# The first image's start: the constants' arithmetic in pieces between x's statistics and transforms, early loads reordered, three Newton steps

## The chip, the cores and the metric

One core of one Trainium2 chip. The metric is the device time of one execution in microseconds; lower is better.

## The reference

The input x has 8 images of 8 channels of 256 x 256 float32 values; the channels form 4 groups of 2. Two layers follow one another:

```python
x = x + fno(group_norm(x))       # 4 Fourier layers between pointwise convolutions
x = x + dilate3x3(group_norm(x)) # maximum over a 3 x 3 window, border -2
```

The Fourier network lifts each group from 2 channels (and 2 coordinate planes) to 10 with a pointwise convolution fc0; runs four layers, each of which adds a spectral convolution (a real 2D FFT, of which only 24 x 12 modes are kept and mixed by complex weights, and the inverse) to a grouped 10 x 10 pointwise convolution; applies `h * sigmoid(h * softplus(beta)) / 1.1` after the first three; and ends with fc1 (128 hidden channels per group), the same swish, and fc2. The group norm divides by `sqrt(var + 1e-5)`, taken over each group of an image. All parameters are inputs of the kernel, so what depends on them alone (softplus of the betas, products of fc0 with the first layer's weights, weights scaled by softplus) is computed on the chip at the start of each execution. That part is called the constants here.

## The kernel before, in words

The Fourier transforms are matrix products with small tables of sines and cosines, so TensorE (PE) does nearly everything: per image, four layers of 11 chunks (`burst` and `transform`), then fc1 and fc2 in 128 steps (`first`, `second`). ScalarE (ACT) applies Silu and copies out of PSUM, VectorE (DVE) transposes, sums and mixes modes, GpSimd (POOL) and SyncE (SP) issue DMAs.

The order of the work on PE, DVE, ACT and SP is written out by hand: inside `tc.manual_schedule` (L931) each of these engines executes its instructions in program order. The pieces of work are Python generators; a `yield` is a place where work of another image can be put between. While an image is in its layers, the head (fc1, fc2) and the tail (`dilate`) of the image before are woven in. The first image has no predecessor, so nothing is woven into its start.

What comes before L931 (the loads L85 to L116, the memsets, the constants L139 to L205) is ordered by a scheduler, which also weaves it into the first instructions of the part written by hand.

The start of an image is `start` (L686): `spectrum_x`, then `mix` for layer 0. For the first image, in order:

- `load_x` (L76, L78): x in two halves of 1 MB, tile `turned`, issued by SP at L85 ahead of all else. L86 to L116 load parameters and tables, some on SP's queue, most on POOL's. The tables that matter below: `grp` (group sums for the statistics of y), `fw` and `er` (transforms of x), `unf`, `fw8` and `stack` (transforms in the layers), `xe`, `wext`. After them SP issues three loads of spectral weights, tile t, 400 KB each (L409), and 44 loads of x in another layout into h (L541, 48 KB each).
- The constants: `softplus` (L139) is called for `beta_p` (4 columns) and `beta_a` (16 columns): an exponential and a logarithm on ACT with small DVE operations around them; `sp` is the softplus, `rs` its reciprocal over 1.1. Then `io` (L160 to L162), fc1's and fc2's weights w1 and w2 scaled (L163, L165), 24 recorded matmuls into `p_wc` (L171, L174), and from these and the softplus `wc` (L176, L179), `wm` (a second use of the tile `wbd`, L182, L184), `cv` (L186) and `cz` (L193 to L198); `wt` (L199) and `wext` (L202) scaled. `wt` is read by the bursts from layer 1 on, w1 and w2 by the head, `wext` by L355, `wc`, `wm` and `cz` at the end of `mix`.
- `spectrum_x` (L275): `bn_stats` of x on DVE, four groups of each half (L281); aggregation (L285); two group means by PE (tiles p_st_x, p_sv_x) with four small DVE operations between and one, L302, behind; the reciprocal square root (`rsqrt`, L258), which is an integer estimate and four Newton steps of three dependent DVE operations each (L263 to L265); x normalized group by group (L306); then matmuls with `er` (L318), a copy (L319), transposes (L324), a copy (L325), matmuls with `fw` (L331), copies (L334), matmuls with `unf` (L343), copies (L347), and on DVE the product with `wext` (L355) and a sum (L358).
- `mix` (L412): twelve large DVE operations (L420, L423) on the modes, small ones, matmuls `p_f` (L464), copies into `fz` (L474 to L480).
- `rows_even` (L483): matmuls `p_g` (L496); their copies into `zt` are shared by DVE and ACT (`copy_banks`, L215 and L217). Then the bursts of layer 0: L600, L606, Silu at L611, transposes at L550, `transform` at L567.

`rsqrt` serves the statistics of x (once an image) and of y (`stats_end`, L229, once an image). For the last image y's statistics and the final dilation (`dilate_last`, L747) come after the last matmul.

Of the kernel before, what the change touches and what calls it, by code (L numbers as in the profile page):

```python
# [21 lines left out]
G = 4  # L22
WID = 10
# [13 lines left out]
NO = 3  # L37
# [9 lines left out]
def fno_dilate_kernel(ctx: ExitStack, tc: tile.TileContext, a: dict, out: bass.AP):  # L47
    nc = tc.nc
    mm = nc.tensor.matmul
# [3 lines left out]
    const = ctx.enter_context(tc.tile_pool(name="const", bufs=1))  # L53
# [8 lines left out]
    def ps_tri(name):  # L62
        return ps.tile([128, 3, 512], F32, tag="tri", bufs=2, name=name)
# [5 lines left out]
    def part(i):  # L69
        return slice(32 * i, 32 * i + 32)  # L70
# [9 lines left out]
    def load(name, shape, eng=nc.gpsimd):  # L80
        t = const.tile(list(shape), F32, tag=f"c_{name}", name=f"c_{name}")
        eng.dma_start(t, a[name])
# [22 lines left out]
    nc.sync.dma_start(wext.rearrange("p g o j -> p (g o j)"), a["wext"].partition_broadcast(128))  # L105
# [7 lines left out]
    w1 = load("w1", (128, NBLK, HID))  # L113
    w2 = load("w2", (128, G, 47))
# [21 lines left out]

    def softplus(t, n, name):  # L139
        e = const.tile([128, n], F32, tag=f"{name}_e", name=f"{name}_e")  # L140
        nc.vector.tensor_scalar(e, t, -1.0, None, ALU.mult)
        nc.vector.tensor_tensor(e, e, t, ALU.max)
        nc.scalar.activation(e, e, AF.Exp, scale=-1.0)
        nc.vector.tensor_scalar(e, e, 1.0, None, ALU.add)
        nc.scalar.activation(e, e, AF.Ln)
        sp = const.tile([128, n], F32, tag=f"{name}_sp", name=f"{name}_sp")
        nc.vector.tensor_scalar(sp, t, 0.0, None, ALU.max)
        nc.vector.tensor_tensor(sp, sp, e, ALU.add)
        nc.vector.tensor_scalar(sp, sp, 1e-20, None, ALU.max)
        rs = const.tile([128, n], F32, tag=f"{name}_rs", name=f"{name}_rs")  # L150
        nc.vector.tensor_scalar(rs, sp, 1.1, None, ALU.mult)
        nc.vector.reciprocal(rs, rs)
        return sp, rs

    sp_p, rs_p = softplus(beta_p, 4, "bp")
    sp_a, rs_a = softplus(beta_a, 4 * G, "ba")
    io = const.tile([128, 4 * G], F32, tag="io", name="io")
    nc.vector.tensor_copy(io[:, 0:4], sp_a[:, 0:4])  # L160
    nc.vector.tensor_tensor(io[:, 4:12], sp_a[:, 4:12], rs_a[:, 0:8], ALU.mult)
    nc.vector.tensor_copy(io[:, 12:16], rs_a[:, 8:12])  # L162
    nc.vector.tensor_scalar(w1, w1, sp_p[:, 3:4], None, ALU.mult)  # L163
    for g in range(G):
        nc.vector.tensor_scalar(w2[:, g, :], w2[:, g, :], rs_a[:, 12 + g : 13 + g], None, ALU.mult)  # L165


    wc = const.tile([128, 32], F32, tag="wc", name="wc")
    p = ps_tri("p_wc")
    for g in range(G):  # L170
        mm(p[32 * g : 32 * g + 6, 0, :32], fc0x[part(g), :], wt[part(g), 0, g, :], start=True, stop=True)  # L171
    for i in range(2):
        for r in range(4):
            mm(p[part(r), 1, NO * G * i : NO * G * (i + 1)], fc0c[:, i, :], wbd[:, NO * r : NO * (r + 1), :],  # L174
               start=True, stop=True)
    nc.vector.memset(wc, 0.0)  # L176
    for g in range(G):
        gs = slice(32 * g, 32 * g + 6)
        nc.vector.tensor_scalar(wc[gs, :], p[gs, 0, :32], sp_p[gs, 0:1], None, ALU.mult)  # L179

    wm = wbd
    nc.vector.memset(wm, 0.0)  # L182
    for g in range(G):
        nc.vector.tensor_scalar(wm[32 * g : 32 * g + 2, :WID, g], wc[32 * g : 32 * g + 2, :WID], -1.0, None, ALU.mult)  # L184
    cv = const.tile([128, 2, NO, G], F32, tag="cv", name="cv")
    nc.vector.tensor_tensor(  # L186
        cv.rearrange("p i o g -> p (i o) g"), p[:, 1, : 2 * NO * G].rearrange("p (i g) -> p i g", g=G),
        sp_a[:, 0:4].unsqueeze(1).to_broadcast([128, 2 * NO, G]), ALU.mult,
    )


    for i, l in enumerate((0, 2)):
        nc.vector.tensor_tensor(  # L193
            cz[:, i], cz[:, i], sp_a[:, 4 * l : 4 * l + 4].unsqueeze(1).to_broadcast([128, NO, G]), ALU.mult,
        )
    nc.vector.tensor_tensor(cz[:, 0], cz[:, 0], cv[:, 0], ALU.add)
    nc.vector.tensor_copy(cz[:, 2], cv[:, 1])
    nc.vector.tensor_scalar(cz1, cz1, sp_p[:, 1:2], None, ALU.mult)  # L198
    nc.vector.tensor_tensor(  # L199
        wt, wt, io.rearrange("p (l g) -> p l g", l=4).unsqueeze(3).to_broadcast([128, 4, G, 32]), ALU.mult,  # L200
    )
    nc.vector.tensor_tensor(  # L202
        wext.rearrange("p g o j -> p g (o j)"), wext.rearrange("p g o j -> p g (o j)"),
        io[:, 0:4].unsqueeze(2).to_broadcast([128, G, 5 * WID]), ALU.mult,
    )  # L205


    alone = [True]

# [48 lines left out]
    def rsqrt(v, r, d):  # L258

        nc.vector.tensor_scalar(r.bitcast(I32), v.bitcast(I32), -0.5, float(0x5F3759DF), ALU.mult, ALU.add)  # L260
        nc.vector.tensor_scalar(v, v, -0.5, None, ALU.mult)
        for _ in range(4):
            nc.vector.tensor_tensor(d, r, r, ALU.mult)  # L263
            nc.vector.tensor_tensor(d, d, v, ALU.mult)
            nc.vector.scalar_tensor_tensor(r, d, 1.5, r, ALU.add, ALU.mult)  # L265
# [663 lines left out]

    stats_of = {}  # L930
    with tc.manual_schedule(engines={PE, DVE, ACT, SP}):  # L931
        d = {}
        for _ in start(0, d):
            pass
        for b in range(n_img):
            stored = [dram.tile([128, NQ * PIX], F32, tag=f"hs{c}", name=f"stored_{b}_{c}") for c in range(NCH)]
            nxt, new, n_ready = {}, None, 0
# [19 lines left out]
            d = nxt  # L957
# [178 lines left out]
```

## Time and profile before

| | |
|---|---|
| median of three runs | 3673.78 us (3665.64, 3673.78, 3674.04) |
| profiled execution | 3669.94 us |
| span of the profile | 3668.1 us |
| mean granted PE clock | 0.979 of full |
| PE busy | 3478.0 us, 95% |
| ACT busy | 2865.8 us, 78% |
| DVE busy | 2388.5 us, 65% |
| x's statistics (L281) on DVE | 9.76 to 16.43 us |
| normalization of x (L306) starts | 26.08 us |
| first burst of layer 0 (L600) starts | 57.79 us |

The table gives times from the start of the span. In the profile a row of the timeline is: start, busy time, engine, line, operation, tiles written and read, their shapes, how often; in brackets the time for which the engine stood idle just before, and what ended that. A wait for several things is put down to the last of them. A row of stages gives from:to, length, then the busy time and count of PE, its weight loads, DVE, ACT and POOL, then the granted PE clock as a share of full speed, the share of the DMA engines and GB/s.

### The profile page before, as it was taken

Reading aid. Unit: us, or ns where it says so; the run is one execution under the profiler, and the core shown is the slowest. Engines: PE = TensorE matmul, PEld = TensorE weight load, DVE = VectorE, ACT = ScalarE, POOL = GpSimd, SP = SyncE. Lnnn points to the kernel's source line nnn. Section 1 sums busy time; section 2 is a strip of 40 time slices with the busy share of each in tenths; the row PEclk is TensorE's granted clock in tenths of the full one; section 3 lists DMA queues with packets and bytes.
Section 4 is the critical chain, followed back from the end, with each engine's and each line's share of the span. In section 5 each row is a group of like instructions: output and inputs, shape, how many; then the busy total and the mean of one; then the engine's idle time right before and its main releaser. Section 6 shows DMA issues by size and latency. Waiting matters only on the chain.

```text
span 3668.1 us, 112640 instructions
## 1 busy us (share of the span) xinstructions
PE 3478.0 (95%) x50872; PEld 1269.3 (35%) x50872; DVE 2388.5 (65%) x3711; ACT 2865.8 (78%) x3021; POOL 117.0 (3%) x202
## 2 busy tenths in 40 slices
PE   5768999999999999999999999999999999999997
PEld 2323333333333333333333333333333333333222
DVE  6776666557775677756776577766777567772443
ACT  2435888888788888787888888888878888879986
POOL 1000000000000000000000000000000000000000
PEclk7879999999999999999999999999999999999998
DMA  3006111442225312271214512253222531225221
GB/s 92 16 16 213 50 50 47 154 119 72 71 87 191 86 52 66 91 223 56 67 56 136 170 56 78 61 174 110 73 72 84 192 85 54 64 70 190 85 81 48
DMA packets 114081, 344.71 MB, mean 94 GB/s; under 512 B 15985, under 2 KB 18481, under 8 KB 98177
## 3 DMA queue, kind: packets, MB, share of 16 engines
q1 hardware_dynamic: 95392, 276.32, 24.8%
q0 software_dynamic: 18208, 61.18, 5.1%
q8 instruction: 400, 6.55, 0.7%
q14 instruction: 81, 0.66, 0.1%
HBM read 213.44 MB, written 123.74 MB: 92 GB/s over the span
## 4 chain that ended last, share of the span: by engine, by line
PE 74%; DVE 15%; issue 5%; ACT 4%; DMA 2%; POOL 0%; ACTq 0%; DVEq 0%; POOLq 0%
PE p_fc L842 20%; PE p_fc L825 20%; PE p_z L606 9%; PE p_d L567 7%; PE p_z L603 7%; PE p_z L600 3%; DVE turned L550 3%; PE p_u L585 3%; DVE y L851 3%; DVE S L423 2%; DVE turned L420 2%; DMA yin<-y_rows 2%; DVE turned L381 1%; PE p_g L518 1%; PE p_b L390 1%
## 5 line engine op out<-in xcount | busy, mean ns | idle before, releaser
L827 ACT ACTIVATE act<-p_fc 128x1536 f32<-128x1536 f32 x1024 | 1493.0, 1458 | 3.1 <-PE p_fc L825 3.1
L825 PE MATMUL p_fc<-hs,c_w 32*128 32x512 f32 x8192 | 1133.3, 626 | 29.8 <-DVE y L851 10.0
L842 PE MATMUL p_fc<-act,c_w 128*32 128x512 f32 x8192 | 1007.5, 599 | 0.2 <-ACT act L827 0.2
L826 ACT ACTIVATE act<-p_fc 128x512 f32<-128x512 f32 x1024 | 616.3, 602 | 214.1 <-PE p_fc L825 201.5
L550 DVE STREAM_TRANSPOSE turned<-h 128x1024 f32<-128x1024 f32 x528 | 632.4, 1225 | 179.0 <-ACT h L611 178.4
L611 ACT ACTIVATE h<-p_z 128x512 f32<-128x512 f32 (+1 forms) x528 | 511.9, 1021 | 205.0 <-PE p_z L606 204.9
L851 DVE TENSOR_TENSOR y<-p_fc,y 128x512 f32<-128x512 f32 x392 | 267.9, 683 | 524.9 <-PE p_fc L842 524.9
L825 PEld LDWEIGHTS p_fc<-hs,c_w 32*128 32x128 f32 x8192 | 356.6, 183 | 602.0 <-ACT act L826 259.2
L842 PEld LDWEIGHTS p_fc<-act,c_w 128*32 128x32 f32 x8192 | 222.5, 109 | 704.7 <-issue 330.7
L606 PE MATMUL p_z<-c_binv,zt 32*128 32x256 f32 x5632 | 410.4, 405 | 0.0
L606 PEld LDWEIGHTS p_z<-c_binv,zt 32*128 32x128 f32 x5632 | 259.3, 186 | 307.5 <-issue 294.4
L603 PE MATMUL p_z<-h,c_wt 32*32 32x512 f32 x8448 | 357.0, 602 | 7.9 <-ACT act L826 4.2
L567 PE MATMUL p_d<-turned,c_fw 32*32 32x480 f32 (+1 forms) x9216 | 308.9, 541 | 0.7 <-DVE turned L550 0.4
L575 ACT ACTIVATE turned<-p_d 128x1440 f32<-128x1440 f32 x144 | 182.9, 1270 | 90.9 <-PE p_d L567 87.6
L613 ACT ACTIVATE h<-p_z,c_bias 128x512 f32<-128x512 f32 (+1 forms) x176 | 186.5, 1110 | 71.7 <-PE p_z L606 71.5
L215 ACT ACTIVATE zt<-p_g 128x198 f32<-128x198 f32 (+2 forms) x118 | 53.6, 576 | 182.1 <-PE p_g L496 98.4
L423 DVE TENSOR_REDUCE S<-turned 128x80 f32<-128x800 f32 x192 | 189.0, 984 | 5.9
L420 DVE TENSOR_TENSOR turned<-t,B 128x800 f32<-128x800 f32 x192 | 188.7, 983 | 1.1
L567 PEld LDWEIGHTS p_d<-turned,c_fw 32*32 32x32 f32 x9216 | 127.3, 103 | 166.0 <-issue 65.0
L381 DVE STREAM_TRANSPOSE turned<-zt 128x960 f32<-128x960 f32 x96 | 177.2, 1873 | 2.5
L603 PEld LDWEIGHTS p_z<-h,c_wt 32*32 32x32 f32 x8448 | 93.2, 103 | 174.4 <-DVE y L851 48.8
L585 PE MATMUL p_u<-turned,c_stack 128*32 128x480 f32 (+1 forms) x1152 | 136.7, 543 | 11.5 <-DVE turned L574 6.2
(198 smaller groups left out, 1754.1 us busy)
## 6 DMA issues: line engine op xcount, KB each, us to landing
stored<-h SPq DMA_DIRECT2D x88, 1024.0 KB
hs<-stored SPq DMA_DIRECT2D x352, 256.0 KB
t<-in_spw SPq DMA_DIRECT2D x96, 400.0 KB
yin<-y_rows POOLq DMA_DIRECT2D x56, 512.0 KB, 5.1
h<-in_xp SPq DMA_DIRECT2D x352, 48.0 KB
turned<-in_xw SPq DMA_DIRECT2D x16, 1024.0 KB
y<-in_x SPq DMA_DIRECT2D x56, 256.0 KB
y_rows<-y POOLq DMA_DIRECT2D x56, 256.0 KB, 4.1
```

What stands on the lines that cost most here:

```text
L420: nc.vector.tensor_tensor(pr, sw[k], bt[:, k2, k].unsqueeze(2).to_broadcast([128, G, 2 * WID, WID]), ALU.mult)
L423: nc.vector.tensor_reduce(s[k2][:, k].rearrange("p s o g -> p (s o) g"), pr.rearrange("p g m i -> p m g i"), AX.X, ALU.add,)
L550: nc.vector.transpose(dst[:, 2 * i : 2 * i + 2], h[:, c, 2 * i : 2 * i + 2].rearrange("p f (s x) -> p f s x", s=2))
L567: mm(banks[q][part(v % 4), : 240 * n], fw8[part(q), v, :], t[part(q), :, :, v, : NBLK * WID], start=v < 4, stop=v >= 4)
L603: mm(o, wt[part(q), l, g, :], h[part(q), c, f, :], start=True, stop=False)
L606: mm(banks[q][:, HW * s : HW * (s + 1)], zt[part(q), 2 * c + s].rearrange("p f o -> p (f o)"), binv[part(q), :], start=False, stop=s == 1)
L611: nc.scalar.activation(dst, src, AF.Silu)
L825: mm(banks[g], w1[part(g), blk, :], hs[k][part(g), :], start=True, stop=True)
L826: nc.scalar.activation(act[:, 0, :], one, AF.Silu)
L827: nc.scalar.activation(act[:, 1:4, :], tri, AF.Silu)
L842: mm(acc[part(g), :], w2[:, g, 15 - rb - i : 47 - rb - i], act[:, g, :], start=i == 0, stop=i == 1)
L851: nc.vector.tensor_tensor(y, sums, y, ALU.add)
```

## The change

Three edits.

1. The loads of `grp`, `fw8` and `stack` on SP's queue move behind the load of `wext`; `fw` moves behind `er`. The other loads keep their order, and POOL's are untouched.
2. The constants become a generator `prepare` with eight pieces, executed inside the part written by hand. `start(0, d)` yields after each of its stages; after its yields 3, 6, 8, 10, 12, 14 and 16 one piece is issued, and the eighth after all of `start`. The arithmetic is the same; the two softplus run side by side, piece by piece.
3. `rsqrt` does three Newton steps in place of four, everywhere.

Where the yields lie: 3 after the aggregation L285; 6 after the operations behind p_st_x (L297); 8 after p_sv_x, the root, and the first group's normalization; 10 after the fourth group's; 12 after L319; 14 after L325; 16 after L334. The matmuls and small operations that follow each yield come behind the piece in the program.

The diff, its core:

```diff
-    grp = load("grp", (128, 128), nc.sync)
-    fw = load("fw", (128, 2, 32), nc.sync)
-    fw8 = load("fw8", (128, 8, 32), nc.sync)
-    stack = load("stack", (128, 32), nc.sync)
     fc0x = load("fc0x", (128, 6))
...
     er = load("er", (128, 2, 32), nc.sync)
+    fw = load("fw", (128, 2, 32), nc.sync)
     unf = load("unf", (128, 3, 32), nc.sync)
...
     nc.sync.dma_start(wext.rearrange("p g o j -> p (g o j)"), a["wext"].partition_broadcast(128))
+    fw8 = load("fw8", (128, 8, 32), nc.sync)
+    stack = load("stack", (128, 32), nc.sync)
+    grp = load("grp", (128, 128), nc.sync)
...
+    def prepare():
+
+        pair = ((beta_p, 4, "bp"), (beta_a, 4 * G, "ba"))
...
+        for i, (t, _, _) in enumerate(pair):
+            nc.vector.tensor_scalar(e[i], t, -1.0, None, ALU.mult)
+            nc.vector.tensor_tensor(e[i], e[i], t, ALU.max)
+        for i in range(2):
+            nc.scalar.activation(e[i], e[i], AF.Exp, scale=-1.0)
+        yield
+        for i, (t, _, _) in enumerate(pair):
+            nc.vector.tensor_scalar(e[i], e[i], 1.0, None, ALU.add)
+            nc.vector.tensor_scalar(sp[i], t, 0.0, None, ALU.max)
+        for i in range(2):
+            nc.scalar.activation(e[i], e[i], AF.Ln)
+        yield
+        p = ps_tri("p_wc")
...
+        yield
+        for i in range(2):
+            nc.vector.tensor_tensor(sp[i], sp[i], e[i], ALU.add)
+            nc.vector.tensor_scalar(sp[i], sp[i], 1e-20, None, ALU.max)
+            nc.vector.tensor_scalar(rs[i], sp[i], 1.1, None, ALU.mult)
+            nc.vector.reciprocal(rs[i], rs[i])
...
+        nc.vector.tensor_tensor(
+            wext.rearrange("p g o j -> p g (o j)"), wext.rearrange("p g o j -> p g (o j)"),
+            io[:, 0:4].unsqueeze(2).to_broadcast([128, G, 5 * WID]), ALU.mult,
+        )
+        yield
+        nc.vector.memset(wc, 0.0)
+        for g in range(G):
+            gs = slice(32 * g, 32 * g + 6)
+            nc.vector.tensor_scalar(wc[gs, :], p[gs, 0, :32], sp_p[gs, 0:1], None, ALU.mult)
+        yield
...
+        nc.vector.memset(wm, 0.0)
...
+        yield
...
+        nc.vector.tensor_scalar(cz1, cz1, sp_p[:, 1:2], None, ALU.mult)
+        yield
+        nc.vector.tensor_tensor(
+            wt, wt, io.rearrange("p (l g) -> p l g", l=4).unsqueeze(3).to_broadcast([128, 4, G, 32]), ALU.mult,
+        )
+        nc.vector.tensor_scalar(w1, w1, sp_p[:, 3:4], None, ALU.mult)
+        for g in range(G):
+            nc.vector.tensor_scalar(w2[:, g, :], w2[:, g, :], rs_a[:, 12 + g : 13 + g], None, ALU.mult)
+        yield
...
-        for _ in range(4):
+        for _ in range(3):
             nc.vector.tensor_tensor(d, r, r, ALU.mult)
...
-        d = {}
-        for _ in start(0, d):
-            pass
+        d, ready = {}, prepare()
+        for n, _ in enumerate(start(0, d), 1):
+            if n in (3, 6, 8, 10, 12, 14, 16):
+                next(ready)
+        next(ready)
```

More of the change, by code (lines that the diff above doesn't have):

```diff
@@ L135, in fno_dilate_kernel @@
     nc.vector.memset(dc, 0.0)
[L139 to L153, printed above, removed]
@@ L157, in fno_dilate_kernel @@
-    sp_p, rs_p = softplus(beta_p, 4, "bp")
-    sp_a, rs_a = softplus(beta_a, 4 * G, "ba")
-    io = const.tile([128, 4 * G], F32, tag="io", name="io")
[L160 to L165, printed above, removed]
@@ L168, in fno_dilate_kernel @@
-    wc = const.tile([128, 32], F32, tag="wc", name="wc")
[L169 to L179, printed above, removed]
+    io = const.tile([128, 4 * G], F32, tag="io", name="io")
@@ L181, in fno_dilate_kernel @@
+    wc = const.tile([128, 32], F32, tag="wc", name="wc")
     wm = wbd
-    nc.vector.memset(wm, 0.0)
-    for g in range(G):
-        nc.vector.tensor_scalar(wm[32 * g : 32 * g + 2, :WID, g], wc[32 * g : 32 * g + 2, :WID], -1.0, None, ALU.mult)
     cv = const.tile([128, 2, NO, G], F32, tag="cv", name="cv")
[L186 to L189, printed above, removed]
@@ L192, in fno_dilate_kernel @@
-    for i, l in enumerate((0, 2)):
+    def prepare():
+        pair = ((beta_p, 4, "bp"), (beta_a, 4 * G, "ba"))
+        e, sp, rs = [[const.tile([128, n], F32, tag=f"{name}_{k}", name=f"{name}_{k}") for _, n, name in pair]
+                     for k in ("e", "sp", "rs")]
+        for i, (t, _, _) in enumerate(pair):
[12 more added lines that the diff above has]
+        for g in range(G):
+            mm(p[32 * g : 32 * g + 6, 0, :32], fc0x[part(g), :], wt[part(g), 0, g, :], start=True, stop=True)
+        for i in range(2):
+            for r in range(4):
+                mm(p[part(r), 1, NO * G * i : NO * G * (i + 1)], fc0c[:, i, :], wbd[:, NO * r : NO * (r + 1), :],
+                   start=True, stop=True)
+        yield
+        for i in range(2):
+            nc.vector.tensor_tensor(sp[i], sp[i], e[i], ALU.add)
+            nc.vector.tensor_scalar(sp[i], sp[i], 1e-20, None, ALU.max)
+            nc.vector.tensor_scalar(rs[i], sp[i], 1.1, None, ALU.mult)
+            nc.vector.reciprocal(rs[i], rs[i])
+        (sp_p, sp_a), (_, rs_a) = sp, rs
+        nc.vector.tensor_copy(io[:, 0:4], sp_a[:, 0:4])
+        nc.vector.tensor_tensor(io[:, 4:12], sp_a[:, 4:12], rs_a[:, 0:8], ALU.mult)
+        nc.vector.tensor_copy(io[:, 12:16], rs_a[:, 8:12])
@@ L193, in fno_dilate_kernel @@
         nc.vector.tensor_tensor(
-            cz[:, i], cz[:, i], sp_a[:, 4 * l : 4 * l + 4].unsqueeze(1).to_broadcast([128, NO, G]), ALU.mult,
-        )
[L196 to L205, printed above, removed]
+            wext.rearrange("p g o j -> p g (o j)"), wext.rearrange("p g o j -> p g (o j)"),
@@ new lines, in prepare @@
+            io[:, 0:4].unsqueeze(2).to_broadcast([128, G, 5 * WID]), ALU.mult,
+        )
+        yield
[5 more added lines that the diff above has]
+        nc.vector.tensor_tensor(
+            cv.rearrange("p i o g -> p (i o) g"), p[:, 1, : 2 * NO * G].rearrange("p (i g) -> p i g", g=G),
+            sp_a[:, 0:4].unsqueeze(1).to_broadcast([128, 2 * NO, G]), ALU.mult,
+        )
@@ new lines, in prepare @@
+        nc.vector.memset(wm, 0.0)
+        for g in range(G):
+            gs = slice(32 * g, 32 * g + 2)
+            nc.vector.tensor_scalar(wm[gs, :WID, g], wc[gs, :WID], -1.0, None, ALU.mult)
+        yield
+        for i, l in enumerate((0, 2)):
+            nc.vector.tensor_tensor(
+                cz[:, i], cz[:, i], sp_a[:, 4 * l : 4 * l + 4].unsqueeze(1).to_broadcast([128, NO, G]), ALU.mult,
+            )
+        nc.vector.tensor_tensor(cz[:, 0], cz[:, 0], cv[:, 0], ALU.add)
+        nc.vector.tensor_copy(cz[:, 2], cv[:, 1])
@@ L208, in fno_dilate_kernel @@
+        nc.vector.tensor_scalar(cz1, cz1, sp_p[:, 1:2], None, ALU.mult)
+        yield
+        nc.vector.tensor_tensor(
+            wt, wt, io.rearrange("p (l g) -> p l g", l=4).unsqueeze(3).to_broadcast([128, 4, G, 32]), ALU.mult,
+        )
+        nc.vector.tensor_scalar(w1, w1, sp_p[:, 3:4], None, ALU.mult)
+        for g in range(G):
+            nc.vector.tensor_scalar(w2[:, g, :], w2[:, g, :], rs_a[:, 12 + g : 13 + g], None, ALU.mult)
+        yield
     alone = [True]
```

## The prediction

> **What bounds the kernel now.** I read the page first, to see how much of the span the change can reach, then the first 60 us in order of time on VectorE (DVE), then the waits of the SP queue, then the granted clock by stage. The page:
>
> ```profile
> span 3668.1 us, 112640 instructions
> PE 3478.0 (95%) x50872; PEld 1269.3 (35%) x50872; DVE 2388.5 (65%) x3711; ACT 2865.8 (78%) x3021; POOL 117.0 (3%) x202
> PE 74%; DVE 15%; issue 5%; ACT 4%; DMA 2%; POOL 0%; ACTq 0%; DVEq 0%; POOLq 0%
> ```
>
> TensorE bounds the whole. But at the front nothing else can run: image 0 has no earlier image to share engines with. PE's first large work, the bursts of layer 0, starts at 57.8 us, and until then the chain runs through DVE. The timeline of DVE, 9 to 27 us (start, busy us, line, tiles):
>
> ```profile
> 9.76 0.69 DVE L281 BATCH_NORM_STATS2 bn_x<-turned 128x6 f32<-128x512 f32 x1
> 11.19 0.16 DVE L148 TENSOR_TENSOR bp_sp<-bp_sp,bp_e 128x4 f32<-128x4 f32 x1 [0.75 <-ACT bp_e L145]
> 13.96 2.47 DVE L281 BATCH_NORM_STATS2 bn_x<-turned 128x6 f32<-128x512 f32 x4
> 16.34 0.41 DVE L285 BATCH_NORM_AGGREGATE mv_x<-bn_x 128x2 f32<-128x12 f32 x4
> 19.37 0.17 DVE L302 TENSOR_SCALAR d_x<-p_sv_x 128x5 f32<-128x5 f32 x1 [0.93 <-PE p_sv_x L272]
> 20.07 0.68 DVE L199 TENSOR_TENSOR c_wt<-c_wt,io 128x512 f32<-128x512 f32 x1
> 20.68 1.02 DVE L179 TENSOR_SCALAR wc<-p_wc,bp_sp 6x32 f32<-6x32 f32 x4
> 24.67 0.41 DVE L163 TENSOR_SCALAR c_w<-c_w,bp_sp 128x384 f32<-128x384 f32 x1
> 25.07 0.70 DVE L165 TENSOR_SCALAR c_w<-c_w,ba_rs 128x47 f32<-128x47 f32 x4
> 25.88 0.17 DVE L265 SCALAR_TENSOR_TENSOR mr_x<-d_x,mr_x 128x5 f32<-128x5 f32 x1
> 26.08 1.53 DVE L306 TENSOR_SCALAR turned<-turned,mr_x 128x1024 f32<-128x1024 f32 x2
> ```
>
> The reader is to see two things. x's statistics (L281) don't begin until the softplus's first steps are through (9.67), and in their midst DVE stands 0.75 us for the logarithm; they end at 16.43. And the constants (L199, L179, L163, L165 and those between) are executed inside the reciprocal root, which lasts from L302 at 19.37 to 26.08. When did x arrive? The SP queue's own waits (total, times, longest):
>
> ```profile
> SPq L105 <- DMA turned<-in_xw: 4.2, 1, 4.2
> SPq L82 <- DMA turned<-in_xw: 0.6, 1, 0.6
> ```
>
> SP's ninth and tenth loads, xe and wext, went out at 5.54 and 10.05, each after a wait for x. x was loaded as two halves ahead of all else, so I read: first half landed by 5.5, second by 10.0. Statistics on the first could have run from 5.5.
>
> Later on DVE stands idle while PE works; the number in brackets is the idle time before the row:
>
> ```profile
> 31.56 0.69 DVE L319 COPY turned<-p_a 128x512 f32<-128x512 f32 x1 [2.29 <-PE p_a L318]
> 33.06 0.69 DVE L325 COPY turned<-p_a 128x512 f32<-128x512 f32 x1 [0.81 <-PE p_a L324]
> 34.92 0.86 DVE L334 COPY turned<-p_a 32x48 f32<-32x48 f32 x4 [1.16 <-PE p_a L331]
> 36.40 0.29 DVE L347 COPY c_xe<-p_xs 128x24 f32<-128x24 f32 x2 [0.62 <-PE p_xs L343]
> 55.41 1.93 DVE L217 COPY zt<-p_g 128x264 f32<-128x264 f32 x4 [1.42 <-PE p_g L496]
> ```
>
> These are the gaps into which the change deals the constants.
>
> **What the Trainium skill says.** "DMA: Bandwidth & Descriptors", section on queues, rings and completion order: on each DMA engine descriptors are consumed in ring order. The trace agrees as far as it shows: x, issued first, landed while later loads were still out; so reordering the loads behind x should not move x. "VectorE: DVE Perf Modes", "The DRAIN you can't avoid": count operations, since a held one waits for the pipe to empty. Here a dependent operation of 0.16 us starts 0.20 after the one before (L263 to L265), an independent one after 0.07 to 0.10. "ScalarE: Activation LUTs", "What ACT_TABLE_LOAD costs": 1.28 us a load and a drain besides; the load here is 1.28 (9.66 to 10.94) and the logarithm starts at 10.95, so no drain is seen. "TensorE: Matmul & The Clock Gate", Part 1: half clock when idle, released after a busy window of some 3.4 us on a free-running grid. The granted clock (third number from the end of a row of stages) fell to half at 37.0 and rose at 77.9:
>
> ```profile
> 60.00:62.00 2.00, 2.00 (x32) 1.23 (x48) 0.00 (x0) 0.50 (x2) 0.00 (x0) 0.50 0.00 0
> 77.50:78.00 0.50, 0.50 (x26) 0.31 (x28) 0.34 (x1) 0.34 (x1) 0.00 (x0) 0.56 0.00 0
> ```
>
> That is 40.9 us, 12 times 3.41, which fits a grid; that 16 us of unbroken matmuls (57.8 to 73.8) did not release it, and only L567's, which follow, did, does not fit "busy" taken as time alone.
>
> **The change, part by part.**
>
> *Statistics first.* The softplus leaves the front, so L281 runs on half 0 from 5.5 to 8.0 (four at 0.62) and on half 1 from 10.05. Four and the aggregation took 13.96 to 16.75, 2.79 us; so they end at 12.85 instead of 16.75: **3.9 us** won. Bounds: nothing, if half 1 really landed at 13.96; 4.5 if SP saw it 0.6 late. I take 3.9.
>
> *Root undisturbed.* At the last image the same root, four steps with nothing between, ran 49.49 to 52.14 (after 3600) from L252 to the next operation: 2.65 us. Three steps: less 3 x 0.195 = 0.585, so 2.07; with five columns its step is 0.20, so 2.1 to 2.2. Before: 26.08 - 19.37 = 6.71. **4.5 us** won, 0.6 of it the fourth step.
>
> *The pieces, where they land.* (1) Four operations ahead of the wait for p_st: two dependent pairs, about 0.65, in a gap of 0.93: nothing; uncovered 0.65. The exponentials follow on ACT (2 x 0.2), idle there. (2) Four independent ones, 0.45, ahead of the wait for p_sv, 0.93: nothing; the exponentials ended about 0.7 us earlier. The logarithm's table load (1.28) and both logarithms run on idle ACT and are wanted 7 us later. (3) 24 small matmuls, 0.6 us on PE, between p_sv and L318, while PE waits for the root: nothing. (4) Eight chained operations at 0.2, three for io at 0.15, wext 0.36, and the memset of L314 (0.2): 2.6 us in the 2.5 from the end of L306 (29.06) to L319: **0.2 lost** (0 to 0.4). (5) A memset of 0.1 and four of 0.25 in 0.81: **0.3 lost**. (6) 0.18 + 0.1 + 4 x 0.17 = 0.95 in 1.16: nothing. (7) Five small ones, 0.65 in 0.62: **0.05**. (8) wt 0.68, w1 0.41, w2 0.70 = 1.8 in 1.42: the first copies of p_g start 0.35 late. Part of that is hidden, since PE's third group waits for ACT's copy too: **0.15** (0 to 0.35). Behind each piece the next DVE instruction queues, and behind it PE. If no gap covered anything, pieces 1, 2 and 4 to 8 would cost some 8 us, the whole gain.
>
> *Loads on SP.* grp, fw8, stack go behind wext; ten loads before and ten after, so the 3 spw and 44 h loads go out as before. er, fw and unf are wanted from 19 us on, fw8 and stack not before 65. Nothing. wext goes out some 5 us earlier. POOL's queue keeps its order.
>
> *Three steps elsewhere.* At the last image's end the root lies on the path: **0.6 us**. In the 14 other roots (seven of x, seven of y) DVE saves 0.6 each beside PE-bound work; the chain at 812 and 2884 us goes through PE there. Nothing; at most DVE's 15% of 8.2, 1.2.
>
> Sum: 3.9 + 4.5 - 0.2 - 0.3 - 0.05 - 0.15 + 0.6 = **8.3 us**. What is late next is PE itself: the bursts begin at about 50 instead of 57.8. The profiled execution took 3669.94 (span 3668.1 and 1.8 around it): 3661.6. That execution lies 3.8 below the median of the three runs and 0.9 below the mean of all four (3670.9, which gives 3662.6). I forecast 3662.
>
> **The rivals.**
>
> A, as above: 3656 to 3667, since executions of the kernel before lie 4 us to either side and the small costs add about 1.5.
>
> B, more: pieces cost nothing (0.7), the clock is released up to 2.7 us of work earlier (dense work runs from L606 at 71.8 to 77.6, a window could fit from 75.2 on; half speed, so 1.4) and the other roots give 1.2: 8.3 + 3.3 = 11.6, 3658.
>
> C, a window missed: the bursts move by 7.7 us against the grid. The window that released the clock, 74.53 to 77.94, was filled with L567 to nine tenths. If none fits, release waits for the next L567, which ended at 85.1: the 7.2 us from 77.9 to there take twice as long, 7 lost: 3669.
>
> D, the order on DVE stays as it was and only the fourth step goes: two roots on the path, 1.2, 3668.7. Against: from L285 on the operations of the spectrum stand in the trace in the order of the program, and the pieces are now part of that program.
>
> E, slower: the same clock stays at half to the end of layer 0. From 77.9 to 103.2 PE did 25.3 us of unbroken work at full clock; at half it takes as much again: 3661.6 + 25.3 = 3687. It decides beyond 8.3 us of such work. Against: L567 comes six times in that layer and is the densest work there.
>
> **How the numbers follow.** A 0.60, B 0.22, C 0.10, D 0.04, E 0.04. About 0.3% (11.0 us) is what a measurement of this kernel can tell from no change: B lies beyond it, A, C and D within, E on the other side. Range 3655 to 3670: it leaves out the ends of A and B and all of E.
>
> **What would show it.** Right: L281 starting at about 5.6 and 10.05; L285 done by 12.9; L302 at 15.5, L306 at 17.7, L355 at about 29, first L600 at about 50; no idle DVE before L319. Wrong: L281 of the second half later than 10.1 (step one); more than 2.3 us from L302 to L306 (step two); more than 0.5 idle on PE added before L324 or L331 (pieces 5, 6); release more than 6 us after the first L567 (C, E).

## The result and the profile after

| | before | after |
|---|---|---|
| median of six runs | 3671.65 us (3665.64 to 3674.04) | 3659.60 us (3656.79 to 3661.23) |
| ratio of the times | | 0.9968 [0.9958, 0.9978] |
| profiled execution | 3669.94 us | 3659.69 us |

The kernel became 12 us faster (8 to 15 by the interval), 0.3%, where 8.3 us were forecast. The two profiled executions lie 10.25 us apart. A second measurement of the same program, `again` below, gave 0.9972 [0.9962, 0.9983] over seven runs.

In the kernel after, lines stand 5 higher: L286 is what L281 was, L311 was L306, L324 was L319, L605 was L600. The page of the kernel after:

```profile
span 3657.9 us, 112591 instructions
PE 3477.2 (95%) x50872; PEld 1268.5 (35%) x50872; DVE 2380.6 (65%) x3663; ACT 2866.5 (78%) x3021; POOL 117.1 (3%) x202
PE 74%; DVE 16%; ACT 4%; issue 4%; DMA 2%; POOL 0%; ACTq 0%; DVEq 0%; POOLq 0%; SPq 0%
```

PE does the same 50872 instructions in 3477.2 us (3478.0 before). DVE has 48 instructions less, 16 roots with three each, and 7.9 us less to do. No engine was relieved of anything that bounds it; what changed is when PE's work could begin. Rows of the first 50 us on DVE, kernel after:

```profile
5.70 2.47 DVE L286 BATCH_NORM_STATS2 bn_x<-turned 128x6 f32<-128x512 f32 x4 [2.52 <-DMA turned<-in_xw]
9.92 2.47 DVE L286 BATCH_NORM_STATS2 bn_x<-turned 128x6 f32<-128x512 f32 x4 [1.75 <-DMA turned<-in_xw]
12.31 0.40 DVE L290 BATCH_NORM_AGGREGATE mv_x<-bn_x 128x2 f32<-128x12 f32 x4
15.34 0.17 DVE L307 TENSOR_SCALAR d_x<-p_sv_x 128x5 f32<-128x5 f32 x1 [0.63 <-PE p_sv_x L277]
17.41 0.16 DVE L270 SCALAR_TENSOR_TENSOR mr_x<-d_x,mr_x 128x5 f32<-128x5 f32 x1
17.61 2.98 DVE L311 TENSOR_SCALAR turned<-turned,mr_x 128x1024 f32<-128x1024 f32 x4
22.82 0.69 DVE L324 COPY turned<-p_a 128x512 f32<-128x512 f32 x1
23.59 1.03 DVE L186 TENSOR_SCALAR wc<-p_wc,bp_sp 6x32 f32<-6x32 f32 x4
24.66 0.69 DVE L330 COPY turned<-p_a 128x512 f32<-128x512 f32 x1
26.51 0.86 DVE L339 COPY turned<-p_a 32x48 f32<-32x48 f32 x4
28.02 0.29 DVE L352 COPY c_xe<-p_xs 128x24 f32<-128x24 f32 x2
46.44 0.70 DVE L210 TENSOR_SCALAR c_w<-c_w,ba_rs 128x47 f32<-128x47 f32 x4
47.05 1.92 DVE L222 COPY zt<-p_g 128x264 f32<-128x264 f32 x4
```

Three things are to be seen. The statistics now wait for x itself (the brackets name its DMA), at 5.70 and 9.92. Between L307 and L311 there is nothing but the root. And the brackets that stood before L319, L325, L334 and L347 are gone: a piece of the constants ends where the copy begins, so that DVE goes from one to the other without a pause. SP's wait for x in the same kernel:

```profile
SPq L82 <- DMA turned<-in_xw: 4.5, 2, 3.9
```

Again SP's ninth and tenth loads wait for x's halves; they are now `stack` (issued at 5.69) and `grp` (9.92). `wext` went out at 4.06 in place of 10.05.

How the lead built up, start before minus start after, each from the same row of both timelines:

| place | before | after | lead |
|---|---|---|---|
| root begins (L302, L307) | 19.37 | 15.34 | 4.03 |
| normalization (L306, L311) | 26.08 | 17.61 | 8.47 |
| copy behind `er` (L319, L324) | 31.56 | 22.82 | 8.74 |
| copy behind the transposes (L325, L330) | 33.06 | 24.66 | 8.40 |
| copies of `p_xs` (L347, L352) | 36.40 | 28.02 | 8.38 |
| first copy of `p_g` (L217, L222) | 55.41 | 47.05 | 8.36 |
| first burst (L600, L605) | 57.79 | 49.41 | 8.38 |
| PE clock full | 77.94 | 68.95 | 8.99 |
| last sum into y (L851, L856) | 3641.92 | 3632.27 | 9.65 |
| span | 3668.1 | 3657.9 | 10.2 |

The clock, kernel after (third number from the end is the granted share):

```profile
66.00:68.00 2.00, 2.00 (x49) 0.92 (x33) 0.00 (x0) 1.40 (x2) 0.00 (x0) 0.50 0.00 0
68.00:70.00 2.00, 2.00 (x63) 0.70 (x31) 0.71 (x2) 0.71 (x1) 0.00 (x0) 0.76 0.00 0
```

0.76 over two microseconds is half speed until 68.95. That is 3.6 us into the first run of L572 (65.38; before it was 4.2 us into L567, from 73.75). In `again`, below, the release came at 68.36, 1.0 us into L572 (from 67.32): it stands at no fixed distance from the work that brings it.

### The profile page after: what moved, and what is told of

Read it like the earlier page. It is cut to its first block, busy times and chain, and to the rows that moved or that the text cites. A ratio compares the mean times of both kernels' runs of the same rounds, so it can differ in the third digit from the quotient of the medians.

```text
span 3657.9 us, 112591 instructions
## 1 busy us (share of the span) xinstructions
PE 3477.2 (95%) x50872; PEld 1268.5 (35%) x50872; DVE 2380.6 (65%) x3663; ACT 2866.5 (78%) x3021; POOL 117.1 (3%) x202
## 4 chain that ended last, share of the span: by engine, by line
PE 74%; DVE 16%; ACT 4%; issue 4%; DMA 2%; POOL 0%; ACTq 0%; DVEq 0%; POOLq 0%; SPq 0%
PE p_fc L847 20%; PE p_fc L830 20%; PE p_z L611 9%; PE p_d L572 7%; PE p_z L608 7%; PE p_z L605 3%; DVE turned L555 3%; PE p_u L590 3%; DVE y L856 2%; DVE S L428 2%; DVE turned L425 2%; DMA yin<-y_rows 2%; DVE turned L386 1%; PE p_g L523 1%; PE p_b L395 1%
## 5 line engine op out<-in xcount | busy, mean ns | idle before, releaser
L856 DVE TENSOR_TENSOR y<-p_fc,y 128x512 f32<-128x512 f32 x392 | 267.6, 683 | 528.7 <-PE p_fc L847 528.7
L611 PE MATMUL p_z<-c_binv,zt 32*128 32x256 f32 x5632 | 409.9, 405 | 0.0
L611 PEld LDWEIGHTS p_z<-c_binv,zt 32*128 32x128 f32 x5632 | 259.0, 186 | 307.0 <-issue 294.1
L608 PE MATMUL p_z<-h,c_wt 32*32 32x512 f32 x8448 | 357.4, 601 | 7.9 <-ACT act L831 4.2
L572 PE MATMUL p_d<-turned,c_fw 32*32 32x480 f32 (+1 forms) x9216 | 308.6, 541 | 0.7 <-DVE turned L555 0.4
L572 PEld LDWEIGHTS p_d<-turned,c_fw 32*32 32x32 f32 x9216 | 127.2, 103 | 165.9 <-issue 65.0
L386 DVE STREAM_TRANSPOSE turned<-zt 128x960 f32<-128x960 f32 x96 | 176.5, 1863 | 2.5
L608 PEld LDWEIGHTS p_z<-h,c_wt 32*32 32x32 f32 x8448 | 93.3, 103 | 174.9 <-DVE y L856 48.8
```

Source lines behind the costliest of these rows:

```text
L572: mm(banks[q][part(v % 4), : 240 * n], fw8[part(q), v, :], t[part(q), :, :, v, : NBLK * WID], start=v < 4, stop=v >= 4)
L608: mm(o, wt[part(q), l, g, :], h[part(q), c, f, :], start=True, stop=False)
L611: mm(banks[q][:, HW * s : HW * (s + 1)], zt[part(q), 2 * c + s].rearrange("p f o -> p (f o)"), binv[part(q), :], start=False, stop=s == 1)
L856: nc.vector.tensor_tensor(y, sums, y, ALU.add)
```

## The experiments

Theory one, from the prediction: the whole gain is the front, worth what the normalization moves, and 0.6 us at the very end; the other 14 roots and the order of the loads are worth nothing. Rivals: the other roots carry a share; the loads do; the clock's release adds to or takes from the front. Each experiment is an edit of the kernel after. The mean of three-step kernels that are the same or nearly so (after, `again` and `loads_before`, 24 runs) is 3660.3 with a standard error of 0.5; means below are compared with it, and ± is one standard error. The mean of the kernel before, over all its 107 runs, is 3671.1. The experiments ran on three chips, on which the kernel before averaged 3670.9, 3671.8 and 3671.1, so that differences of 1 us between them are not read.

**Statistics behind the softplus again.** `softplus_first`:

```diff
+        next(ready)
+        next(ready)
         for n, _ in enumerate(start(0, d), 1):
-            if n in (3, 6, 8, 10, 12, 14, 16):
+            if n in (8, 10, 12, 14, 16):
                 next(ready)
```

> The changed kernel with pieces 1 and 2 (the softplus up to its logarithm) issued ahead of x's statistics. Theory: DVE waits for beta_a until 9.0 and for the exponentials until 9.9, and the eight operations of statistics then run through without a wait: aggregation ends at 15.2 instead of 12.7, L311 starts at about 20.1, the first burst at 51.9, the whole 2.5 us slower (3662). Rival: what held the statistics of the kernel before was not the order but x itself; then L311 stays within 0.5 of 17.6.

Measured: median 3664.36 over 13 runs, 0.9980 [0.9972, 0.9988]; mean 3664.2 ± 0.6, so 3.9 ± 0.8 slower than with the statistics first (3.3 by the kernel before on the same chip); 2.5 was expected. DVE in `softplus_first`:

```profile
7.45 0.17 DVE L150 TENSOR_SCALAR bp_e<-c_beta_p 128x4 f32<-128x4 f32 x1 [4.27 <-DMA c_beta_p<-in_beta_p]
...
9.17 0.17 DVE L150 TENSOR_SCALAR ba_e<-c_beta_a 128x16 f32<-128x16 f32 x1 [1.35 <-DMA c_beta_a<-in_beta]
10.00 4.84 DVE L286 BATCH_NORM_STATS2 bn_x<-turned 128x6 f32<-128x512 f32 x8
14.76 0.41 DVE L290 BATCH_NORM_AGGREGATE mv_x<-bn_x 128x2 f32<-128x12 f32 x4
20.05 1.53 DVE L311 TENSOR_SCALAR turned<-turned,mr_x 128x1024 f32<-128x1024 f32 x2
```

What holds x's statistics back here is less arithmetic than waiting: the first instruction of each softplus stands at the head of DVE's queue until its parameters have landed, `beta_p` at 7.45 and `beta_a`, 16 columns, at 9.17. x's first half, there by 5.70, waits behind them. When DVE gets to x, nearly all of it is there, and the eight run without a gap. The normalization starts at 20.05, 2.44 us later than in the kernel after. The first burst then came at 53.71, 4.3 later than in the profile after; `again`, below, says where the other 1.9 come from.

**All other pieces in one block ahead of the root.** `pieces_at_root`:

```diff
-            if n in (3, 6, 8, 10, 12, 14, 16):
+            if n in (3, 6):
                 next(ready)
-        next(ready)
+            if n == 7:
+                for _ in range(6):
+                    next(ready)
```

> The changed kernel with pieces 3 to 8 issued together just ahead of the root of x, so that nothing covers them. Theory: DVE's pieces 4 to 8, 6.4 us by the durations in the changed kernel's trace, all lie on the path, less the 0.4 that they cost where they are: L311 starts 6.2 us later (23.8), the first burst 5.9 later (55.3), the whole about 6 us slower (3665.6). Rival: later stages have slack, so that the first burst starts under 2 us later.

Measured: median 3665.28 over 13 runs, 0.9987 [0.9978, 0.9995]; mean 3665.8 ± 0.6, 5.5 slower than in pieces. DVE in `pieces_at_root`:

```profile
20.88 0.70 DVE L210 TENSOR_SCALAR c_w<-c_w,ba_rs 128x47 f32<-128x47 f32 x4
21.49 0.15 DVE L307 TENSOR_SCALAR d_x<-p_sv_x 128x5 f32<-128x5 f32 x1
23.76 2.98 DVE L311 TENSOR_SCALAR turned<-turned,mr_x 128x1024 f32<-128x1024 f32 x4
```

Pieces 3 to 8 hold L307 up from 15.34 to 21.49, 6.15 us; between them in the gaps they cost next to nothing. This is the cover that the prediction named. The parts don't add up: 6.15 for these pieces, 2.44 for the softplus with its waits and 0.58 for the fourth step (`four_steps`) make 9.2, where the normalization moved by 8.47. In the kernel before, some of the pieces ran between the root's own steps, where each cost less than its length: L163, 0.41 us long, put the next step off by 0.21, and L165, 0.70 long, by 0.49.

**The same program again**, to see what a single execution can tell. `again` has no edit.

> The changed kernel once more, to have its time beside the other runs on this chip: 3659.6 within 1.5 us, and in the front the eight matmuls L323 take between 4.3 and 5.7 us, as the clock's phase has it.

Measured: median 3659.84 over seven runs, mean 3659.9 ± 1.0. Its front is not that of the first profile. PE, kernel after:

```profile
18.52 4.26 PE L323 MATMUL p_a<-turned,c_er 128*32 128x512 f32 x16 [2.70 <-issue]
49.41 2.01 PE L605 MATMUL p_z<-h,wcn 6*32 6x512 f32 x32
```

PE, `again`:

```profile
18.60 5.63 PE L323 MATMUL p_a<-turned,c_er 128*32 128x512 f32 x16 [2.70 <-issue]
51.36 2.01 PE L605 MATMUL p_z<-h,wcn 6*32 6x512 f32 x32
```

The same sixteen matmuls, started within 0.1 us of each other, took 4.26 in one execution and 5.63 in the other. In the thirteen profiles of this front they took from 4.26, in the kernel after, to 5.71, and 4.52 in the kernel before; the transforms L336 behind them took 1.07 to 1.91. The durations of the single records say why (shortest, median and longest in ns); kernel after:

```profile
L323 PE MATMUL p_a<-turned,c_er x16: 592/754/1062, 18.5 to 22.2; 128*32 128x512 f32 x16
```

`again`:

```profile
L323 PE MATMUL p_a<-turned,c_er x16: 947/1061/1062, 18.6 to 23.3; 128*32 128x512 f32 x16
```

At image 1, where the granted clock is full, the same records take 592. Here they begin at 1062, half speed or little more, and in the kernel after they become 592 on the way, in `again` they don't. The clock's records, which the column of the granted clock is made of, begin only with a first change, to full, at 21.16 us in the profile after and at 23.99 in `again`; the 1.00 that the column shows ahead of that is not borne out by these durations. So the first release falls into these matmuls early or late, 2.8 us apart for the same program. A first burst at 49.4 or at 51.4 thus belongs to the same program, and the lead of 8.38 in the table is 6.4 if `again` stands for after. The rest of the late burst of `softplus_first` (L323 5.17, L336 1.85, against 4.26 and 1.07) is this, not the softplus.

**The old order of the loads.** `loads_before` puts the loads of `grp`, `fw`, `fw8` and `stack` back where they were:

```diff
+    grp = load("grp", (128, 128), nc.sync)
+    fw = load("fw", (128, 2, 32), nc.sync)
+    fw8 = load("fw8", (128, 8, 32), nc.sync)
+    stack = load("stack", (128, 32), nc.sync)
     fc0x = load("fc0x", (128, 6))
...
-    fw = load("fw", (128, 2, 32), nc.sync)
...
-    fw8 = load("fw8", (128, 8, 32), nc.sync)
-    stack = load("stack", (128, 32), nc.sync)
-    grp = load("grp", (128, 128), nc.sync)
```

> The changed kernel with the loads in the order of before (grp, fw, fw8, stack ahead of er). Theory: nothing, within 1.5 us of 3659.6, both halves of x land as before at about 5.5 and 10.0, wext goes out at about 10 and is there before it is wanted at 22. Rival: the early loads bring part of the gain; then x's second half or wext comes later and L311 starts over 0.5 us later than 17.6.

Measured: median 3660.67 over 11 runs, 0.9973 [0.9964, 0.9982]; mean 3661.1 ± 0.9; against the 13 runs of after and `again` alone (3659.7 ± 0.6) that is 1.5 ± 1.0 slower, not told apart from nothing. DVE and SP in `loads_before`:

```profile
5.80 2.47 DVE L286 BATCH_NORM_STATS2 bn_x<-turned 128x6 f32<-128x512 f32 x4 [2.62 <-DMA turned<-in_xw]
10.24 2.47 DVE L286 BATCH_NORM_STATS2 bn_x<-turned 128x6 f32<-128x512 f32 x4 [1.96 <-DMA turned<-in_xw]
```

```profile
10.23 0.33 SPq L105 DMA_DIRECT2D c_wext<-in_wext  x1
```

`wext` is late again, and nobody misses it. x's second half lands 0.3 us later and the normalization starts at 17.92. That is at the edge of what the order of the loads can be said to do: in the ten profiles with the new order in which DVE is free for the second half, it starts on it at 9.83 to 10.03.

**Four steps everywhere.** `four_steps` puts `range(4)` back into `rsqrt`.

> The changed kernel with four Newton steps in every root, as before the change; the rest as changed. Theory: only the first and the last root lie on the path, so it is 1.2 us slower than the changed kernel (some 3661), L311 starts at 18.2 instead of 17.6, and between first burst and the last matmul nothing changes. Rival: the 14 other roots count too, at DVE's 15% of the chain or more: 2.4 us or up to 9 slower (3662 to 3669).

Measured: median 3663.36 over 21 runs, 0.9980 [0.9974, 0.9987]; mean 3663.4 ± 0.5, 3.1 ± 0.7 slower than with three. The normalization starts at 18.19, 0.58 later, as priced; the root at the end gives 0.59 (2.66 against 2.07 us). That leaves two microseconds, and so the other 14 roots came under suspicion.

**The fourteen other roots alone**, with eight steps, then with four:

```diff
-    def rsqrt(v, r, d):
+    def rsqrt(v, r, d, steps):
...
-        for _ in range(3):
+        for _ in range(steps):
...
-        rsqrt(v, r, d)
+        rsqrt(v, r, d, 3 if name == f"y{n_img - 1}" else 8)
...
-        rsqrt(d[:, 1], mr[:, 1], d[:, 0])
+        rsqrt(d[:, 1], mr[:, 1], d[:, 0], 3 if b == 0 else 8)
```

> The changed kernel, but the 14 roots other than the first of x and the last of y do eight Newton steps, five more than now: 70 steps, 41 us of DVE time. Theory: these roots are hidden beside PE; the time stays within 1.5 us of the changed kernel's 3659.6. Rival: they lie on the path with DVE's share of the chain, 15%, which gives 6 us more (3666); if all of it counted, 41 more (3700).

Measured: median 3670.68 over 13 runs, 1.0000 [0.9992, 1.0008]; mean 3670.4 ± 0.9, 10 us slower for 70 added steps (41 us on DVE). Both theories fell: it is neither hidden nor DVE's share of the chain. The trace says why. Behind a root DVE stands idle before its next wanted work. Kernel before, an x root and a y root:

```profile
712.72 0.69 DVE L851 TENSOR_TENSOR y<-p_fc,y 128x512 f32<-128x512 f32 x1 [1.45 <-PE p_fc L842]
815.92 1.25 DVE L550 STREAM_TRANSPOSE turned<-h 128x1024 f32<-128x1024 f32 x1 [0.79 <-ACT h L611]
```

Kernel after, the same two places:

```profile
703.66 0.69 DVE L856 TENSOR_TENSOR y<-p_fc,y 128x512 f32<-128x512 f32 x1 [2.06 <-PE p_fc L847]
806.89 1.25 DVE L555 STREAM_TRANSPOSE turned<-h 128x1024 f32<-128x1024 f32 x1 [1.38 <-ACT h L616]
```

The idle time grew by 0.61 and 0.59: the saved step was absorbed. That slack, 1.4 to 2.1 us, is also all that more steps can use up. Five more steps are 2.95 us, and what exceeds the slack lands on PE: in `others_eight` DVE's idle time behind y's roots is 0.05 us, and the lag against the kernel after grew from 4 us in image 1 to 13 in the last, some 1.5 us an image. Five steps were the wrong size of experiment here: they ran past the cover whose existence was in question. So the same edit with 4 for 8, `others_four`:

> The changed kernel, but the 14 roots other than the first of x and the last of y do four steps, as before the change. Theory: in the trace DVE's idle time behind these roots grew by just the step that was saved (1.46 to 2.06 behind the roots of x, 0.79 to 1.38 behind those of y), so they were hidden; the time is that of the changed kernel, at most 0.6 more for image 1's root, which the normalization follows at once. Rival: the four-step kernel was 3 to 4 us slower than the changed one where 1.2 was expected, so these roots cost 2 us or more.

Measured: median 3662.96 over 21 runs, 0.9979 [0.9973, 0.9986]; mean 3663.3 ± 0.5, 3.0 ± 0.7 slower than three steps. One root of the 14 explains a part. Image 1's x root comes while image 0 is still in its layers; nothing is put between the root and the transforms, and PE's `er` matmuls follow normalized group by normalized group. That row (before: L318), in the kernels before, after, `others_four`, `two_steps` (next) and `others_eight`:

```profile
309.46 3.27 PE L318 MATMUL p_a<-turned,c_er 128*32 128x512 f32 x16
```

```profile
300.67 2.67 PE L323 MATMUL p_a<-turned,c_er 128*32 128x512 f32 x16
```

```profile
302.72 3.26 PE L323 MATMUL p_a<-turned,c_er 128*32 128x512 f32 x16
```

```profile
301.59 2.06 PE L323 MATMUL p_a<-turned,c_er 128*32 128x512 f32 x16
```

```profile
304.25 4.03 PE L323 MATMUL p_a<-turned,c_er 128*32 128x512 f32 x16 [1.57 <-ACT h L618]
```

3.27, 2.67, 2.06 with four, three and two steps: 0.6 us a step, on PE, and with eight steps 1.36 more and 1.57 idle ahead. (A busy PE row includes the time in which its matmuls are held up within the group.) In images 2 to 7 the same row takes 1.92 or 1.93 us in all of these kernels: their roots don't reach it. The rest of the 3 us is less clear. In the profile of `others_four` the clock falls to half for 3.4 us at 351 us:

```profile
350.00:360.00 10.00, 10.00 (x138) 3.96 (x132) 5.32 (x5) 7.64 (x8) 0.00 (x0) 0.83 0.50 113
```

In `again` it doesn't:

```profile
350.00:360.00 10.00, 10.00 (x206) 4.24 (x192) 5.75 (x6) 9.14 (x10) 0.00 (x0) 1.00 0.54 127
```

A mean of 0.83 over 10 us is 1.7 us lost. That window is no mark of four steps. Windows like it come in layer 0 of images 1 to 7, in other images in each execution (the last section shows when): two in the profile after, three in `again` and in `others_four`, four in `four_steps`, but four in `two_steps` too. The start of the row L323 shows what the other roots did in this execution. `others_four` lies 0.1 us behind `again` at image 1, 3.1 at image 2 and 0.65 at image 7. Of the 3.0 gained between images 1 and 2, 0.6 is image 1's root, 1.7 the window, and 0.6 a pause within L608 that is 0.9 us here and 0.3 in `again`; from there to image 7 nothing was added that lasted. So the traces place 0.6 of the mean's 3.0 ± 0.7 at a root, and where the rest lies is open.

**Two steps everywhere.** `two_steps` has `range(2)`, which makes the root less exact.

> The changed kernel with two Newton steps in every root. Theory: 1.2 us faster than the changed kernel (first and last root, 0.6 each), at most 1.8; L311 starts at 17.0. Rival: every step counts 3 to 4 us over all 16 roots, then 3656.

Measured: median 3660.66 over seven runs, 0.9971 [0.9961, 0.9982]; mean 3659.4 ± 1.0, so -0.9 ± 1.1 against three steps: neither the front's and the end's 1.2 nor nothing at all is excluded. In its profile the normalization starts at 16.94, 0.67 earlier, and image 1's row is 0.6 shorter, as above.

**The half clock of layer 0.** In all these kernels PE's clock falls to half ahead of `mix`; in the kernel after it is back at 68.96, so that PE's work from the first burst on, 19.5 us, runs at half speed. That is 9.8 us of clock, the most that a full clock could give there. Three kernels keep PE busy there with matmuls whose results nobody reads. `warm_layer0` adds three large ones behind each of six products in layer 0's `mix`, while image 0 is alone; `warm_all` does so in its layers 1 to 3 too and adds 24 behind the transposes L386; `warm_light` takes 33 smaller ones in image 0's layers 1 to 3 only. The edit of the first two, cut to `mix`; `KEEP` is (0,) in one and (0, 1, 2, 3) in the other:

```diff
+                if alone[0] and l in KEEP:
+                    if n == 0:
+                        keep = ps_a(f"p_keep_{b}_{l}")
+                    for _ in range(3):
+                        mm(keep, avg, turned[:, 2, 1024 * k2 : 1024 * k2 + 512], start=True, stop=True)
```

> The changed kernel with 18 matmuls more, whose results nobody reads: during the mix of the first image's layer 0, three of 128 x 128 x 512 follow each of the six products, on operands that are there, while PE has nothing to do. Theory: dense work releases PE's clock at about 36 to 40, and it then stays at full through the bursts: p_g, four bursts and L572 run at full speed, which is worth about 8 to 10 us (3650). Rival: the work of L605 (6 of 32 rows) does not count as activity, so the clock falls back within 7 us of the first burst, and the gain is under 4 us (3656 or more). Second rival: the added matmuls delay p_f, and the start of L501 comes later than 45.7.

> As with the added matmuls in layer 0's mix, and the same in the mix of layers 1 to 3 of the first image and two after each of its four transposes in layers 1 to 3 (24 more), again read by nobody. Theory: the clock then never falls in the first image; half speed in layers 1 to 3 of the changed kernel lasted from about 104 to 133, 182 to 212 and likewise in layer 3, in each of which about 5 us of half-speed matmuls are on the path: 7 to 10 us less than with layer 0 alone (3640 to 3645). Rival: the matmuls delay DVE, whose next transposes or products overwrite what they read; then layers 1 to 3 gain nothing or lose.

Measured: `warm_layer0` 3695.09 over five runs, 1.0066 [1.0052, 1.0080]; `warm_all` 3703.06 over four, 1.0087 [1.0073, 1.0101]. PE and DVE in `warm_layer0`:

```profile
34.51 17.14 PE L432 MATMUL p_keep<-turned,avg 128*128 128x512 f32 x36 [4.66 <-DVE turned L426]
325.07 2.81 PE L432 MATMUL p_keep<-turned,avg 128*128 128x512 f32 x6 [2.08 <-DVE turned L426]
```

```profile
38.81 0.99 DVE L426 TENSOR_TENSOR turned<-t,B 128x800 f32<-128x800 f32 x1 [1.51 <-PE p_keep L432]
```

and its clock, around the first burst (56.5):

```profile
57.00:58.00 1.00, 1.00 (x36) 0.21 (x8) 0.26 (x1) 0.98 (x3) 0.00 (x0) 0.96 0.00 0
58.00:60.00 2.00, 2.00 (x32) 1.24 (x46) 0.00 (x0) 1.24 (x2) 0.00 (x0) 0.50 0.00 0
```

The clock was full from 37 us on, through the rest of `mix`, and it did not help: 1.5 us into the first bursts, at 57.92, it fell to half and stayed there to 75.0. PE was busy at that moment, but it had stood idle for 1.4 us up to 55.81, so that this fall alone doesn't say whether the idle time or the bursts brought it about. The added matmuls were also too large: each is two records, 0.9 us together at full clock, and since they read `turned`, DVE's next product waits for them (the 1.51). And the edit reached further than meant: the flag that says image 0 is alone is still set when image 1 starts, so image 1's `mix` got 18 as well (the row at 325), and a lag of 8 us against the kernel after there became 23. What a front at full clock would be worth can't be read from these two.

> The changed kernel with 33 matmuls more in layers 1 to 3 of the first image, read by nobody: two behind each of the first three transposes of spectrum_h, one (80 columns of weights) behind each of the first five sums of mix, on operands that DVE doesn't overwrite soon. Theory: PE's clock stays at full into the matmuls p_b, p_f and p_g of these layers, which now run at half; 3 to 4 us less in each layer, 3650 in all. Rival: the clock falls in the mix none the less, or the added matmuls delay p_b and p_f: no gain or a loss.

Measured: 3672.27 over 13 runs, 1.0002 [0.9994, 1.0010], 11.6 slower by the means (3671.9 ± 0.7) than three steps. Layer 1 of image 0 in `warm_light`:

```profile
128.00:134.00 6.00, 3.79 (x225) 3.24 (x226) 3.10 (x12) 0.92 (x3) 0.00 (x0) 1.00 0.23 70
```

and in `again`:

```profile
128.00:134.00 6.00, 4.53 (x219) 4.34 (x224) 2.71 (x11) 0.50 (x2) 0.00 (x0) 0.57 0.23 70
```

Here the clock is full where it was at 0.57, and PE does as many matmuls in 3.79 us as it did in 4.53. But it was idle for 2.2 and 1.5 us of that stretch: what the clock gave went into waiting, and layer 1 ended no earlier. Up to layer 2's matmuls `p_f` (L469) 2.5 us were lost against `again`, and the lag grew to 9 in later images, which run none of the added matmuls. Why is not settled.

## Why the prediction was right, and where not

*Statistics first*, 3.9: right. The statistics' aggregation ended at 12.71 in place of 16.75, 4.04 us. They began at 5.70 and 9.92 (said: 5.5 to 5.6 and 10.05). The cause was only half read: the prediction spoke of the softplus's steps and the logarithm (0.75). `softplus_first` shows that what stands ahead of the exponentials makes 2.4 of the 4.0, most of it the two waits for `beta_p` and `beta_a`; in the kernel before they ended at 6.79 and 9.01.

*Root undisturbed*, 4.5: right. L307 to L311 took 2.27 us, 4.44 less; 0.58 of it is the fourth step (`four_steps`). Together the two moved the normalization by 8.47; 8.4 was forecast.

*The pieces.* Each cost as little as priced, or less. (4): at L324 the lead is 8.74, more than at L311, since the matmuls took 4.26 and not 4.52; DVE is never idle from L311 to L324, so the piece just fits. (5): 8.74 to 8.40, **0.34** (0.3). (7): **0.03** (0.05). (8): 0.15 was priced, and 0.02 to 0.03 lost: the first copies start at 47.05 on DVE and 47.02 on ACT. `pieces_at_root` shows that this was the cover and not cheapness: the same pieces uncovered cost 5.5 to 6 us.

*Loads on SP*, nothing: right within 0.3 us at the front; in the whole, 1.5 ± 1.0 doesn't exclude a small share (`loads_before`).

*Three steps elsewhere.* The last root gave 0.58: right. "In the 14 other roots [...] DVE saves 0.6 each beside PE-bound work [...] Nothing": **this sub-step failed for one of them.** It holds in the traces for the x roots of images 2 to 7, whose L323 takes 1.92 us with any number of steps, and for y's, where the idle time behind each of the seven grew by 0.58 or 0.59. For image 1's x root the saving goes to PE, 0.6 us. The prediction had read the chain at 812 and 2884 us, and took those for all.

*The clock.* It was released 3.6 us into L572, so neither C nor E came, and B's "up to 2.7 us of work earlier" was 0.6. In the ten profiles without added matmuls the release came 0.9 to 4.2 us into that first run, so that C's missed window, 7 us, was never met.

*The sum.* For the profiled pair it is 8.4 at the first burst, 0.6 at image 1's root and 0.6 at the end, 9.6 of 10.2. That the remainder is small is in part luck: some 15 us behind image 1's root PE pauses 0.57 us in the kernel after and not in the kernel before, which takes 0.5 of the lead back, and another 1.1 is gained in small amounts that no experiment placed. Half-speed windows after 340 us are no part of it, since both profiles have the same three, at the same places of the program. It is luck too that the profile after has the shortest `er` matmuls of all thirteen; with `again` in its place the lead at the first burst is 6.4, where the prediction's terms gave 7.7. For the means, 3671.1 and 3660.3, the gain is 10.8 ± 0.6 against 8.3 forecast. A holds as the mechanism; in the profiled pair its sum was 0.3 short at the pieces, 0.3 at the clock of the `er` matmuls (4.26 against 4.52 us) and 0.6 at image 1. What lies between 9.6 and 10.8 has not been shown. The 12.05 us of the medians and the 10.8 of the means lie on both sides of the 11.0 that the prediction took as the limit of what can be told from no change, so its likeliest case, within that limit, is neither confirmed nor refuted by the amount; that the kernel is faster is certain.

The ends of the range had been set by executions of the kernel before that lie 4 us to either side. (It was said to leave out the ends of A; A's 3656 to 3667 lie inside it.) That was sound: six runs after span 4.4 us, 21 of `others_four` 8.6, and the front alone moves by 2 us with the clock's phase.

## What to carry to other kernels

An instruction that waits for a small late load, put ahead of ready work on an engine whose order is written out, holds up all of it: here, in `softplus_first`, 16 columns of parameters kept a megabyte waiting that had landed 3.5 us before. Work that must be done anyway cost next to nothing in pieces no longer than the gaps in which DVE waited for PE (0.6 to 2.5 us here), and its full length in one block. When a saving is repeated over many instances, look at each kind of instance, the first one above all: the root of image 1 had nothing between it and PE's matmuls, and the slack behind its thirteen siblings said nothing of it.

## What the runs showed of the hardware

The Trainium skill ("TensorE: Matmul & The Clock Gate", Part 1) has the clock at half when PE is idle and released by a busy window of some 3.4 us, the windows running freely. The runs agree on the grid: in each of ten profiles all changes of the clock lie within 0.04 us of a grid of 3.41 us, and its phase differs from execution to execution. They add that being busy isn't enough. In the kernel after, 16 us of unbroken work in layer 0's bursts (49.41 to 65.38) did not bring the clock back, and L572 did, 0.9 to 4.2 us after its start in the ten profiles. These bursts are L605, whose weights are 6 rows by 32 columns, in turn with L611, 32 by 128; L572's are 32 by 32.

The same bursts also take the clock away where PE is never idle. L605 alone in the kernel after, in two windows of the grid and in the window behind each (from:to, length, PE busy and count, weight loads, clock, DMA share, GB/s):

```profile
1645.91:1649.32 3.41, 2.40 (x64) 0.51 (x62) 1.00 0.02 5
1649.32:1652.73 3.41, 0.03 (x2) 0.00 (x0) 0.50 0.00 0
345.45:348.86 3.41, 2.12 (x63) 0.30 (x36) 1.00 0.41 89
348.86:352.27 3.41, 0.00 (x0) 0.00 (x0) 1.00 0.39 82
```

PE works through all four without a gap. L605 fills 2.40 us of the first, and the clock is at half in the next; it fills 2.12 of the third, and the clock stays. In the ten profiles without added matmuls there are 24 such falls between 300 and 3490 us. In the window before each, L605 fills 2.27 to 2.41 us; in no other window of that stretch at full clock does it fill more than 2.17. Where the grid lies decides whether a window catches that much of two bursts, and so which images are struck: one to four falls in an execution, 1.7 us of clock for each window at half. This is a description of these bursts; what it is in L605 that counts for little, its 6 rows above all, was not varied. The runs of one kernel scatter with a standard deviation of 1.4 to 3.2 us. Windows at half and the front's phase, up to 2 us, are of that size; that they are all of it is not shown. An estimate from that scatter: to tell 2 us takes ten runs or more of each kernel.

A ninth and a tenth load on SP's queue did not go out until the first and the second, x's halves, had landed: 5.54 and 10.05 before, 5.69 and 9.92 after. `xe`, `stack`, `wext` and `grp` all waited so when they stood ninth or tenth.

A float32 matmul of 128 x 128 weights with 512 columns is two records and took 0.90 us at full clock (12 records in 5.42 us in image 1 of `warm_layer0`).
